# Thirty-two series of unused matmuls behind the last step: two row tiles with other column counts and places, then one row tile alone with other operands

## The chip, the core and the metric

The kernel runs on one core of one Trainium2 chip. A core has five engines with queues of their own: TensorE (PE in the profile; its weight loads stand apart as PEld), VectorE (DVE), ScalarE (ACT), GpSimd (POOL) and SyncE (SP, which here only issues DMAs). The metric is the device time of one execution in microseconds, the median of several runs. One run is also profiled, and all rows quoted below come from that one.

## The reference

The network has four residual layers on an image batch `x` of shape (4, 32, 32, 16). Three of them are alike: a group norm, then a layer in which every output pixel (i, j) has its own 3x3 convolution kernel.

```python
first   = einsum('ijyx,byxc->bijc', M, x)
shifted = conv(x, G[i, j], 3x3, 'SAME')            # for every one of 1024 pixels (i, j)
diff    = relu(x - shifted)
second  = einsum('ijyx,bijyxc->bijc', W, diff)
x       = x + first - second
```

With 1024 pixels, 16 output channels, four images and 1024 positions, `shifted` has 67 million elements for each of the three layers. That is where nearly all the time goes. The layer between the second and the third of them is a small interval-pooling network.

## The kernel before, in words

The batch is cut into two groups of two images, so there are six phases (three layers by two groups). A phase has eight chunks of 128 pixels, and a chunk has 32 steps, one for each of the 16 channels and two images. That makes 1536 steps. One step computes, for 128 pixels at once, the convolution at all 1024 positions of one image: a PSUM tile of 128 x 2 x 512 fp32, two banks, called `pc`.

The two halves of the tile (index `h`) belong to the left and right half of the image. Half `h` takes its operands from partitions 64h to 64h+63, so each matmul has 64 rows and 128 columns of weights, and the two halves work on two different row tiles of TensorE. The code issues them in turn, `h` = 0 and then `h` = 1, for each pair of operands (`products`, L629).

The operands are typed `float32r`, which the profile prints as f32. To come near fp32 precision, the inputs and weights are split into high and low parts, and seven products are accumulated in each step: two with `ib` and two with `ia` (`first_part`), then, after ScalarE has scaled the PSUM tile in place (L665), two with `iyz` and one with `im9` (`second_part`). The `ib` and `iyz` products have 512 columns, `ia` and `im9` 496 (the last or first image column is left out). After that, VectorE reads the PSUM tile, takes the minimum with zero, multiplies it by the pixel weights and sums it into an accumulator (L682). The first 16 steps (the units below `PLAIN`) take true fp32 operands `raw` in place of the split ones; such a product is two records in the profile.

The order is written out by hand (`manual_schedule`). The loop in `conv_layer` opens the first part of a step before the second part of the one before it, and lets background work in between (the preparation of weights in `prep_parts`, the group norm and gathers of the next phase in `behind`). PSUM tiles come in turn from four pairs of banks (`bank_pair`, tag `ps`, 4 buffers), so a new tile has to wait until the reader of the tile four allocations earlier is done. Weights of a unit of four channels lie in a tile `parts` of 2 x 3 x 4 x 128 columns; `ib[0]` holds 2048 columns of inputs of the first group.

At the end, the last `second_part` runs alone, VectorE adds the last accumulator to `X[1]` (L700), and SyncE sends the last slice of `X[1]` to the output (L904). Then all engines meet at a closing barrier.

## Time and profile before

| | us |
|---|---|
| median of 2 runs | 2481.81 (2479.29 and 2484.33) |
| time of the profiled execution | 2481.97 |
| its span, first to last instruction | 2480.3 |
| TensorE busy | 2458.5 (99%), 21906 matmuls |
| TensorE weight loads | 2074.2 (84%) |
| VectorE busy | 2086.0 (84%) |
| ScalarE busy | 1878.2 (76%) |
| GpSimd busy | 1579.3 (64%) |
| granted TensorE clock, mean | 1.000 |

Matmuls are pipelined: a record's duration covers its way through the array too, and it overlaps the next one's. How fast TensorE goes is therefore read from the distance between the starts of neighbouring matmuls and not from a matmul's duration. In the timeline view, neighbours of one kind are merged into one line (x4 is four matmuls, two on each row tile), and the first column is the start of the first of them.

### The profile page before, as it was taken

The page shows a single profiled execution, that of the slowest core. Times are in us where ns is not written, and L with a number is a line of the kernel's source. Part 1 is how long each engine was busy: PE and PEld are TensorE (multiplying, and loading weights), DVE is VectorE, ACT ScalarE, POOL GpSimd, SP SyncE. Part 2 cuts the span into 40 slices and gives each one's busy share as a digit, 9 for nine tenths or more (in the row PEclk, how much of TensorE's full clock was granted, in tenths as well). Part 3 has the DMA queues.
Part 4 walks back from the last instruction along what each step waited for, and adds up shares of the span by engine and source line. Part 5 has one row for each costly group of instructions (what it writes and reads, how often), then busy time and mean ns, then how long its engine had stood idle before and what let it go on. Part 6 is the DMA issues. An engine that isn't in the chain of part 4 may idle for free.

```text
span 2480.3 us, 58060 instructions
## 1 busy us (share of the span) xinstructions
PE 2458.5 (99%) x21906; PEld 2074.2 (84%) x21906; DVE 2086.0 (84%) x3617; ACT 1878.2 (76%) x2181; POOL 1579.3 (64%) x1750
## 2 busy tenths in 40 slices
PE   8999999999999999999999999999999999999999
PEld 4888888888888888888888989888989888888887
DVE  8888878888888888788898988899889888788887
ACT  3778767787777778677777777787777787677776
POOL 4766655667555667555567777586778676555552
PEclk9999999999999999999999999999999999999999
DMA  6556744465454457544454545574455477554442
GB/s 189 140 144 183 213 131 134 138 180 157 137 145 137 137 157 193 176 137 137 137 145 119 143 126 139 146 195 124 129 139 145 120 187 201 150 145 137 137 137 54
DMA packets 97673, 366.92 MB, mean 148 GB/s; under 512 B 26480, under 2 KB 31472, under 8 KB 97392
## 3 DMA queue, kind: packets, MB, share of 16 engines
q1 hardware_dynamic: 95696, 361.57, 52.9%
q8 instruction: 172, 2.82, 0.5%
q10 hardware_dynamic: 1568, 1.62, 0.3%
q14 instruction: 109, 0.89, 0.1%
q0 software_dynamic: 128, 0.02, 0.0%
HBM read 199.78 MB, written 1.02 MB: 81 GB/s over the span
## 4 chain that ended last, share of the span: by engine, by line
PE 94%; DVE 2%; DMA 2%; issue 1%; ACT 1%; POOL 0%; SPq 0%; ACTq 0%; DVEq 0%; POOLq 0%
PE pc L629 92%; DVE junk L682 1%; PE pf L427 1%; DMA parts<-parts 1%; ACT pc L665 0%; DMA raw<-in_xi 0%; DMA raw<-in_g 0%; DMA ia<-first 0%; PE ps_l L550 0%; DMA first<-in_g 0%; PE ps_r L563 0%; DVE tables L510 0%; DVE raw L848 0%; DVE upper_w L203 0%; SPq L302 0%
## 5 line engine op out<-in xcount | busy, mean ns | idle before, releaser
L682 DVE SCALAR_TENSOR_TENSOR junk<-pc,WT 128x1024 f32<-128x1024 f32 x1536 | 1880.0, 1224 | 363.6 <-PE pc L629 316.8
L665 ACT ACTIVATE pc<-pc 128x1024 f32<-128x1024 f32 x1520 | 1531.8, 1008 | 556.1 <-PE pc L629 531.6
L629 PE MATMUL pc<-ib,parts 64*128 64x512 f32 x6080 | 953.0, 387 | 4.7 <-DVE junk L682 2.9
L629 PE MATMUL pc<-iyz,parts 64*128 64x512 f32 x6080 | 950.3, 387 | 5.3 <-ACT pc L665 5.2
L629 PE MATMUL pc<-ia,parts 64*128 64x496 f32 x6080 | 928.5, 379 | 0.0
L629 PEld LDWEIGHTS pc<-ib,parts 64*128 64x128 f32 x6080 | 585.1, 184 | 109.3 <-DVE junk L682 8.5
L629 PEld LDWEIGHTS pc<-ia,parts 64*128 64x128 f32 x6080 | 587.6, 184 | 106.2
L629 PEld LDWEIGHTS pc<-iyz,parts 64*128 64x128 f32 x6080 | 586.2, 184 | 94.9 <-ACT pc L665 9.4
L629 PE MATMUL pc<-im,W 64*128 64x496 f32 x3072 | 606.4, 384 | 0.0
L237 POOL TENSOR_TENSOR parts<-raw,upper_w 128x512 fp32r<-128x512 f32 x190 | 249.0, 1311 | 496.3 <-DVE upper_w L203 447.3
L629 PEld LDWEIGHTS pc<-im,W 64*128 64x128 f32 x3072 | 297.8, 184 | 57.3 <-issue 3.6
L243 POOL CAST parts<-parts 32x512 fp32r<-32x512 f32 x380 | 231.2, 608 | 48.8 <-ACT parts L240 30.5
L238 POOL TENSOR_TENSOR W<-W,raw 128x512 fp32r<-128x512 f32 x190 | 246.9, 1300 | 7.8 <-ACT W L175 7.8
L241 POOL TENSOR_TENSOR parts<-parts 128x512 fp32r<-128x512 f32 x190 | 246.5, 1297 | 2.2 <-ACT parts L236 2.0
L245 POOL CAST parts<-upper_w 32x512 fp32r<-32x512 f32 x380 | 231.6, 609 | 22.8
L214 POOL TENSOR_TENSOR raw<-raw,ident 128x512 f32<-128x512 f32 x190 | 199.5, 1050 | 61.5 <-DMA raw<-in_g 36.6
L175 ACT ACTIVATE W<-raw,low_w 128x512 fp32r<-128x512 f32 x190 | 136.2, 717 | 9.2 <-DMA ia<-first 9.2
L682 DVE DVE_READ_ACCUMULATOR junk<-pc,WT 128x1 f32 x1536 | 127.8, 83 | 0.0
L236 ACT ACTIVATE parts<-upper_w 128x512 fp32r<-128x512 f32 x190 | 118.8, 625 | 4.8 <-DVE upper_w L203 4.7
L240 ACT CAST parts<-upper_w 128x512 fp32r<-128x512 f32 x190 | 116.6, 614 | 0.0
L697 POOL TENSOR_SCALAR acc<-acc 128x32 f32<-128x32 f32 x40 | 16.7, 417 | 136.5 <-DVE junk L682 134.6
L203 DVE TENSOR_SCALAR upper_w<-raw 128x512 int32<-128x512 int32 x190 | 85.2, 449 | 2.7 <-POOL raw L214 2.3
(139 smaller groups left out, 479.1 us busy)
## 6 DMA issues: line engine op xcount, KB each, us to landing
raw<-in_g SPq DMA_DIRECT2D x190, 768.0 KB, 7.1
parts<-parts SPq DMA_DIRECT2D x380, 384.0 KB, 5.0
WT<-in_w SPq DMA_DIRECT2D x48, 512.0 KB, 4.6
MT<-in_mt SPq DMA_DIRECT2D x24, 512.0 KB, 7.9
raw<-xs SPq DMA_DIRECT2D x120, 71.8 KB, 3.1
ib<-temp SPq DMA_DIRECT2D x40, 128.0 KB, 2.4
ia<-temp SPq DMA_DIRECT2D x80, 62.0 KB, 3.4
raw<-in_xi SPq DMA_DIRECT2D x3, 287.0 KB, 5.0
```

Source lines behind the costliest of these rows:

```text
L175: nc.scalar.activation(dst, src, AF.Copy, scale=mask[:, 1:2])
L214: eng.tensor_tensor(raws[u][:, s, at:to], raws[u][:, s, at:to], pick[s][:, f0 + at : f0 + to].unsqueeze(2).to_broadcast([P, to - at, P]), ...
L236: nc.scalar.activation(WD, high, AF.Copy, scale=-EPS)
L237: nc.gpsimd.tensor_tensor(WL, w8, high, ALU.subtract)
L238: nc.gpsimd.tensor_tensor(W9, W9.bitcast(F32), src[:, 2], ALU.add)
L240: nc.scalar.copy(WU, high)
L241: nc.gpsimd.tensor_tensor(WD, WD.bitcast(F32), WL.bitcast(F32), ALU.add)
L243: nc.gpsimd.tensor_copy(WU[hi], WL[lo].bitcast(F32))
L245: nc.gpsimd.tensor_copy(WL[lo], high[hi])
L629: nc.tensor.matmul(ps[:, h, at : at + n], lhsT=w[r], rhs=v[r] if n == NH else v[r][:, :n], start=first and k == 0, stop=k == len(pairs) - ...
L665: nc.scalar.activation(ps, ps, AF.Copy, scale=1.0 + EPS)
L682: nc.vector.scalar_tensor_tensor(junk, ps.rearrange("p h n -> p (h n)"), 0.0, chunks[n], op0=ALU.min, op1=ALU.mult, accum_out=accs[phase][ ...
```

## The change

After the output has been issued, 32 series of further matmuls are put into TensorE's queue. Each series takes a new PSUM tile and writes the same place of it 14 or 20 times (`start=True, stop=True`, so nothing accumulates). Nobody reads these tiles. The weights are slices of the last unit's `parts` tile, the moving operand is slices of `ib[0]`; both are left over from the kernel's own work.

- Twelve series (`aa` to `al`) of 20 pairs go to both row tiles in turn, as the kernel's own products do. They differ in the column count `n` (512, 480, 464, 448, 488, 504) and in which columns of `ib[0]` and `parts` the operands start.
- Twenty series (`ba` to `bt`) of 14 matmuls go to the first row tile alone. Among them are fewer weight columns (`m` of 64, 32, 96), weights whose access pattern repeats one column or half of them, moving operands whose pattern repeats 256, 64 or 16 columns or each column 16 times, the same operands each time, and column counts from 256 to 512.

In all that is 480 + 280 = 760 matmuls, each with its weight load. The rest of the program is left as it is, but for a list that keeps the last `parts` tile within reach.

```diff
+    all_parts = [None]
...
             parts = wpool.tile([P, 2, 3, FU, P], F32R, tag="parts", bufs=AHEAD + 1, name=f"parts_{u}")
             W9 = wpool.tile([P, FU, P], F32R, tag="W9", bufs=AHEAD + 1, name=f"W9_{u}")
+            all_parts[0] = parts
...
     second_part(*open_steps.pop(0))
     nc.sync.dma_start(out[1][:, NT - 1], X[1][:, NT - 1])
 
+    xf = ib[0].rearrange("p s b n -> p (s b n)")
+    wf = all_parts[0].rearrange("p a k f n -> p (a k f n)")
+
+    def more(name, n=NH, m=P, xs=(0, 512), ws=(0, 128), po=0, tiles=(0, 1), wc=None, xc=None, count=20):
+        ps = bank_pair(f"more_{name}_")
+        for k in range(count):
+            x0, w0 = xs[k % len(xs)], ws[k % len(ws)]
+            for h in tiles:
+                r = slice(64 * h, 64 * h + 64)
+                w, x = wf[r, w0 : w0 + m], xf[r, x0 : x0 + n]
+                if wc:
+                    w = bass.AP(w.tensor, w.offset, [list(w.ap[0])] + wc)
+                if xc:
+                    x = bass.AP(x.tensor, x.offset, [list(x.ap[0])] + xc)
+                nc.tensor.matmul(ps[:m, h, po : po + n], lhsT=w, rhs=x, start=True, stop=True)
+
+    one = dict(tiles=(0,), count=14)
+    more("aa")
+    more("ab", n=480)
+    more("ac", n=480, xs=(0,))
+    more("ad", n=480, xs=(0,), ws=(0,))
+    more("ae", n=480, xs=(0,), ws=(128,))
+    more("af", n=480, xs=(512,), ws=(0,))
+    more("ag", n=480, xs=(0, 256))
+    more("ah", n=480, xs=(0, 512, 1024, 1536), ws=(0, 256))
+    more("ai", n=464, xs=(0,), ws=(0,))
+    more("aj", n=448, xs=(0,), ws=(0,))
+    more("ak", n=488)
+    more("al", n=504)
+    more("ba", **one)
+    more("bb", m=64, **one)
+    more("bc", m=32, **one)
+    more("bd", m=96, **one)
+    more("be", wc=[[0, P]], **one)
+    more("bf", wc=[[64, 2], [1, 64]], **one)
+    more("bg", n=480, **one)
+    more("bh", n=464, **one)
+    more("bi", n=496, **one)
+    more("bj", n=448, **one)
+    more("bk", n=256, **one)
+    more("bl", n=384, **one)
+    more("bm", xc=[[0, 2], [1, 256]], **one)
+    more("bn", xc=[[0, 8], [1, 64]], **one)
+    more("bo", xc=[[0, 32], [1, 16]], **one)
+    more("bp", xc=[[1, 512 // 16], [0, 16]], **one)
+    more("bq", m=64, ws=(0, 64), **one)
+    more("br", xs=(0,), ws=(0,), **one)
+    more("bs", n=508, **one)
+    more("bt", n=498, **one)
```

## The prediction

> **What bounds the kernel now.** I read three views: the page for the bound, the timeline for the distance between matmuls, and the end of the timeline for what the added work can hide. On the page, the first line gives busy shares, the clock row gives the granted clock in 40 slices (9 is 90% or more), and the next line is the chain that ended last.

> ```profile
> PE 2458.5 (99%) x21906; PEld 2074.2 (84%) x21906; DVE 2086.0 (84%) x3617; ACT 1878.2 (76%) x2181; POOL 1579.3 (64%) x1750
> PEclk9999999999999999999999999999999999999999
> PE 94%; DVE 2%; DMA 2%; issue 1%; ACT 1%; POOL 0%; SPq 0%; ACTq 0%; DVEq 0%; POOLq 0%
> ```

> TensorE is the bound from end to end, at full clock. Work put behind its last matmul cannot hide behind another engine, except in the short tail. So the question is the price of one matmul of each kind. One steady step, TensorE alone, in the timeline (start, length, line, kind, count):

> ```profile
> 2471.39 0.38 PE L629 MATMUL pc<-im,W 64*128 64x496 f32 x2
> 2471.61 0.62 PE L629 MATMUL pc<-ib,parts 64*128 64x512 f32 x4
> 2472.06 0.60 PE L629 MATMUL pc<-ia,parts 64*128 64x496 f32 x4
> 2472.50 0.62 PE L629 MATMUL pc<-iyz,parts 64*128 64x512 f32 x4
> 2472.96 0.38 PE L629 MATMUL pc<-im,W 64*128 64x496 f32 x2
> ```

> The reader is to see starts: from 2471.39 to 2472.96, seven pairs pass in 1.57 us, four of 512 columns and three of 496. In the records' own start times (ns), a pair of 512 is followed after 226 or 227, a pair of 496 after 220 (1185 of 2050 `ia` to `ia` distances, the commonest value by far). The 16 columns between them cost 6.7 ns, so a column costs 1/2.4 ns, and each pair has 13.4 ns on top: 512/2.4 + 13.4 = 226.7, 496/2.4 + 13.4 = 220.1.

> This price belongs to **one tile**, not to the pair. In stretches where the two tiles run apart by 30 ns, the distances alternate 30 and 197 (512) or 30 and 190 (496): again 227 and 220 for each tile, whatever the other does.

> **The two-tile series.** Twelve series of 20 pairs. The column counts are 512 (`aa`), seven times 480 (`ab` to `ah`), 464, 448, 488 and 504, together 5776. So 20 x (5776/2.4 + 12 x 13.4) = 20 x (2406.7 + 160.8) = 51,350 ns: **51.3 us**. I cost other columns, shared columns and repeated weights at nothing, because `ia`, `ib`, `iyz` and `im` lie at different places and keep the same rule. A gain is bounded by the 13.4 ns (3.2 us in all); a loss has no row.

> **The one-tile series.** Twenty series of 14: twelve of 512 (6144), and 480, 464, 496, 448, 256, 384, 508 and 498 (3534), together 9678 columns. The trace before has one product on the first row tile alone, `ps_r` (L563), true fp32 in two passes:

> ```profile
> 1331.70 0.38 PE L629 MATMUL pc<-im,W 64*128 64x496 f32 x2
> 1331.70 0.40 PEld L563 LDWEIGHTS ps_r<-tables,r 64*128 64x128 f32 x2
> 1331.92 0.75 PE L563 MATMUL ps_r<-tables,r 64*128 64x352 f32 x2
> ...
> 1334.25 0.36 PE L563 MATMUL ps_r<-tables,r 64*128 64x231 f32 x1
> ...
> 1334.44 0.36 PE L563 MATMUL ps_r<-tables,r 64*128 64x231 f32 x1
> ```

> Its passes start 295 ns apart at 352 columns and 195 at 231, which is 1/1.2 ns a column plus 2 to 3. The fp32 products on both tiles (`raw`) start 430 apart at 512 columns: the same rate. So a tile alone is neither faster nor slower than one of two, in the one type where the trace shows both. The second weight load of `ps_r` starts 2 ns after the first pass and is covered by it.

> I therefore take the float32r rule for the lone tile as well: 14 x (9678/2.4 + 20 x 13.4) = 14 x (4032.5 + 268) = 60,210 ns: **60.2 us**. From below, the nearest rows bound the extra at 2.7 ns (`pf`, fp32, 256 columns: starts 216 apart against 213.3), which for all 520 slots (240 pairs, 280 singles) would take 5.6 us off. From above, two prices, both rivals below: the load in the open, and the fp32 column rate. I take 13.4, the row of the same type and shape.

> Smaller terms. A weight load that nothing covers moves the next matmul by 108 ns (at 2475.33 below: 335 instead of 227), so a load needs about 108; at 256 columns (`bk`) the slot is 120, and it still fits. Fewer weight columns (`bb`, `bc`, `bd`, `bq`) can only shorten the load; the change of tile width costs about 0.1 us where the trace has one (`im` to the 32-column `ps_l`, 317 instead of 220 ns), under 1 us for about seven. Repeating patterns (`be`, `bf`, `bm` to `bp`): the trace shows moving operands in runs of 16 (`raw`) at the common fp32 rate, but none that repeats. A form at half rate would cost 14 x 213 = 3 us, so 0 to 12 us if the four moving ones all did; I take 0, as short runs cost nothing.

> **Waits.** The four pairs of PSUM banks go round. The last four steps' readers end at about 2473.1, 2474.7, 2476.2 and 2477.6; the first four series begin at about 2476.1, 2480.7, 2485 and 2489, after each of them. From `ae` on, the previous writer of the buffer is TensorE itself, three series (10 us) back, and writing one place again is what every accumulating product does without a wait. Operands have long been there.

> **The end.** These are the last rows before:

> ```profile
> 2475.33 0.73 PE L629 MATMUL pc<-iyz,parts 64*128 64x512 f32 x4 [0.43 <-ACT pc L665]
> 2475.67 0.19 PEld L629 LDWEIGHTS pc<-im,W 64*128 64x128 f32 x2
> 2475.90 0.39 PE L629 MATMUL pc<-im,W 64*128 64x496 f32 x2
> 2476.15 0.08 DVE L682 DVE_READ_ACCUMULATOR junk<-pc,WT 128x1 f32 x1
> 2476.39 1.23 DVE L682 SCALAR_TENSOR_TENSOR junk<-pc,WT 128x1024 f32<-128x1024 f32 x1 [0.16 <-PE pc L629]
> 2477.54 0.08 DVE L682 DVE_READ_ACCUMULATOR junk<-pc,WT 128x1 f32 x1
> 2477.66 0.19 DVE L700 SCALAR_TENSOR_TENSOR X<-acc,X 128x32 f32<-128x32 f32 x1
> 2477.88 0.35 SPq L904 DMA_DIRECT2D out<-X  x1
> ```

> The output lands 1.4 us after its issue, at 2479.28, and the closing barrier takes the 1.0 us to 2480.3. The first added pair can start at 2475.90 + 0.22 = 2476.12. So VectorE's last reduction and the output (2476.12 to 2479.28, 3.2 us) lie beside added matmuls and drop from the path; if that cover were gone, they would cost those 3.2 us.

> **Sum.** 2476.12 + 51.35 + 60.21 = 2587.68; the last matmul's results come 0.2 us after its slot (length 0.39 in a slot of 0.22); plus 1.0 us of closing: span 2588.9. The profiled execution's time is 1.7 above its span (2481.97 against 2480.3), so **2590.5 us**, 108.5 above its own 2481.97, which is 0.16 above the median of the runs shown. The order of everything earlier is as before, so I take nothing from it.

> [...]

> **Rivals.**
> - *Lone loads in the open.* On two tiles, one tile's load could be covered by the other's stream, a cover that the lone tile lacks. Price: 280 x 108 = 30.2 us, so 2620.7. Against it: `ps_r`, and the tiles that run apart at an unchanged 227. For it: `ps_r` is the only lone row, with two passes of one product. Chance 0.07.
> - *A lone tile at half rate*, through the port that feeds it or a clock that drops when half of the array rests (the trace shows no long stretch of that kind). 14 x 9678/1.2 + 280 x 2.7 = 113.7 in place of 60.2: 2644. Chance 0.06.
> - *Some forms dearer, or waits between series*: four repeated forms at half rate 12 us, tile-width changes 1 us, so 2594 to 2606. Chance 0.13.
> - *Not slower: the unread matmuls are dropped* when the program is compiled, since no instruction reads a `more` tile. Then none of the 760 records appears, and the time is 2482. It decides at one point: whether an instruction without a reader is kept. In the trace nothing speaks for dropping, but it also has no unread tile. Chance 0.02.

> **Numbers.** The forecast, 2584 to 2594 by the bounds of the extra, has 0.70; the rest, 0.02, goes to cheaper ones. The range 2582 to 2606 takes in the forecast and the dearer forms (0.83), and leaves out open loads, half rate and dropping. A measurement of this kernel tells about 2% (50 us) from no change, so every case but dropping is slower: 0.98.

> **What would show it.** 760 more matmuls on TensorE's line of the page, about 111.6 us of new span after 2476. Right: 226.7 ns between `aa` pairs, 213.4 between the 480 ones, 227 between lone `ba` matmuls, and the output issued at 2477.9 as before. Wrong: lone matmuls about 335 apart (open loads) or 427 (half rate), a granted clock below 1 in the second half of the added stretch, or gaps at the starts of series.

## The result and the profile after

The changed kernel takes 2593.74 us, the median of 2 runs (2593.00 and 2594.49), against 2481.81 before: a ratio of 1.0448, with a 95% interval of 1.0430 to 1.0465. The forecast was 2590.5 us. The profiled execution takes 2593.0 us with a span of 2591.3.

From the page of the changed kernel, the rows that answer to those shown of before (busy shares, granted clock in 40 slices, the chain that ended last; the lines of the old code have moved down by one or two):

```profile
PE 2571.8 (99%) x22666; PEld 2166.7 (84%) x22666; DVE 2087.9 (81%) x3617; ACT 1878.4 (72%) x2181; POOL 1578.8 (61%) x1750
PEclk9999999999999999999999999999999999999999
PE 94%; DVE 2%; DMA 2%; issue 1%; ACT 1%; POOL 1%; SPq 0%; ACTq 0%; DVEq 0%; POOLq 0%
```

All 760 matmuls are there (21906 became 22666). The busy time of the other engines is unchanged within 2 us, and the clock is full in every slice.

The timeline of the changed kernel around the old end (start, length, engine, line, operation, count):

```profile
2476.79 0.39 PE L631 MATMUL pc<-im,W 64*128 64x496 f32 x2
2476.80 3.17 PEld L922 LDWEIGHTS more_aa__32783<-ib,parts 64*128 64x128 f32 x28
2477.02 3.36 PE L922 MATMUL more_aa__32783<-ib,parts 64*128 64x512 f32 x27
...
2478.55 0.19 DVE L702 SCALAR_TENSOR_TENSOR X<-acc,X 128x32 f32<-128x32 f32 x1
2478.77 0.35 SPq L906 DMA_DIRECT2D out<-X  x1
```

The first added matmul starts 0.23 us after the last `im` pair, where 0.22 lie between them in the steady steps. The last reduction and the output go on beside the added work. Two windows of the same trace, the twelve two-tile series and the twenty lone ones (length, then busy time and instruction count of each engine, granted clock, DMA share, GB/s; matmuls under way at a window's edge are counted too):

```profile
2477.02:2529.24 52.22, 52.22 (x482) 44.93 (x479) 1.53 (x5) 0.00 (x0) 0.00 (x0) 1.00 0.01 2
2529.24:2590.16 60.92, 60.92 (x282) 47.43 (x279) 0.00 (x0) 0.00 (x0) 0.00 (x0) 1.00 0.00 1
```

The forecast had 51.35 and 60.21. The lone series can be read one by one in TensorE's timeline; the distance from one line's start to the next, over 14, is the slot of one matmul:

```profile
2529.24 3.36 PE L922 MATMUL more_ba__33275<-ib,parts 64*128 64x512 f32 x14
2532.44 3.39 PE L922 MATMUL more_bb__33290<-ib,parts 64*64 64x512 f32 x14
...
2548.60 3.19 PE L922 MATMUL more_bg__33365<-ib,parts 64*128 64x480 f32 x14
2551.63 3.10 PE L922 MATMUL more_bh__33380<-ib,parts 64*128 64x464 f32 x14
...
2560.49 1.83 PE L922 MATMUL more_bk__33425<-ib,parts 64*128 64x256 f32 x14
2562.16 2.59 PE L922 MATMUL more_bl__33440<-ib,parts 64*128 64x384 f32 x14
...
2570.99 3.54 PE L922 MATMUL more_bo__33485<-ib,parts 64*128 64x512 f32 x14
2574.37 3.18 PE L922 MATMUL more_bp__33500<-ib,parts 64*128 64x512 f32 x14
2577.39 3.38 PE L922 MATMUL more_bq__33515<-ib,parts 64*64 64x512 f32 x14
```

From these, `ba` has 228 ns, `bg` 217, `bk` 120, and `bo` (runs of 16 that repeat) 242. `bp` (each column 16 times) has 216, less than any other of 512 columns. Two of the paired series, from the critical chain of the same trace (start, length, count):

```profile
2481.75 4.33 PE more_ab__32824 L922 x40
2512.08 4.20 PE more_ai__33111 L922 x40
```

Over their 20 pairs that is 216.7 ns at 480 columns and 210 at 464, the same as the lone `bg` and `bh`. Each series begins one slot after the last matmul of the one before (`bk` 203 ns after the last of `bj`, whose slot is 203; `bl` 120 after the last of `bk`), so the change of PSUM tile costs nothing here.

### The profile page after: what moved, and what is told of

It is laid out like the page before. It is cut to its first block, busy times and chain, and to the rows that moved or that the text cites. A ratio compares the mean times of both kernels' runs of the same rounds, so it can differ in the third digit from the quotient of the medians.

```text
span 2591.3 us, 59580 instructions
## 1 busy us (share of the span) xinstructions
PE 2571.8 (99%) x22666; PEld 2166.7 (84%) x22666; DVE 2087.9 (81%) x3617; ACT 1878.4 (72%) x2181; POOL 1578.8 (61%) x1750
## 4 chain that ended last, share of the span: by engine, by line
PE 94%; DVE 2%; DMA 2%; issue 1%; ACT 1%; POOL 1%; SPq 0%; ACTq 0%; DVEq 0%; POOLq 0%
PE pc L631 88%; DVE junk L684 1%; PE pf L429 1%; DMA raw<-in_g 1%; DMA parts<-parts 1%; DMA raw<-in_xi 0%; ACT pc L667 0%; PE more_aa__32783 L922 0%; PE more_al__33234 L922 0%; PE more_ak__33193 L922 0%; PE ps_l L552 0%; PE more_ah__33070 L922 0%; PE more_ae__32947 L922 0%; PE more_ag__33029 L922 0%; PE more_af__32988 L922 0%
```

## The experiments

In every kernel here the network itself is computed in full. Only the unused series change, or where they stand.

### Each half alone

```diff
     more("aa")
     ...
     more("al", n=504)
-    more("ba", **one)
-    ...
-    more("bt", n=498, **one)
```

> Only the twelve two-tile series are left (aa to al). My theory, a slot price for each matmul of a tile and a fixed cover of about 3 us by the tail: the series take the same 52.2 us as in the changed kernel (2477.02 to 2529.24), and the time is about 2481.8 + 52.2 - 3.0 = 2531 us. Rival (most of the added time comes from the lone series, the paired ones are partly free): under 2520 us.

> Only the twenty series on one row tile are left (ba to bt). My theory: the same 60.9 us as in the changed kernel, so about 2481.8 + 60.9 - 3.0 = 2540 us, lone 512-column matmuls 227 to 229 ns apart, granted clock 1.0. Rival (a tile alone is slower, or lowers the clock, once nothing on two tiles runs just ahead of it): 2560 us or more, and a clock below 1 in the stretch.

With the paired series alone the time is 2532.1 us (median of 4), 1.0193 of before (1.0178 to 1.0208); with the lone ones alone 2542.6, 1.0232 (1.0216 to 1.0248). The kernel before had a median of 2483.4 beside them. The series take 52.2 and 60.9 us in these traces too, and the plain lone 512-column matmuls (`ba`) are 226 to 236 ns apart, 229 in the mean, at full clock. Both halves cost what they cost in the changed kernel, and neither depends on the other.

### The series ahead of the last second part

```diff
+    ps = bank_pair("more_all_")
+    ... all 32 series, into this one tile ...
     second_part(*open_steps.pop(0))
     nc.sync.dma_start(out[1][:, NT - 1], X[1][:, NT - 1])
```

> All 32 series, but put ahead of the last step's second part, so that the last reduction and the output come after them; they share one PSUM tile. My theory (the tail is covered in the changed kernel and would be on the path here): from the start of the last but one step's im pair to the end of the span, 5.8 us before and 115.9 in the changed kernel, it is about 5.8 + 113.1 - 0.7 = 118.2 us, the 0.7 being the wait for ScalarE and the uncovered load that the series now hide. Rival (the tail hid nothing, the closing needs it anyway): 115.9 us or less.

The first two lines of this kernel's timeline below are the `im` pair of the last but one step and the first added pair, the others the end:

```profile
2474.12 0.38 PE L631 MATMUL pc<-im,W 64*128 64x496 f32 x2
2474.34 0.39 PE L920 MATMUL more_all__32773<-ib,parts 64*128 64x512 f32 x2
...
2588.41 1.23 DVE L684 SCALAR_TENSOR_TENSOR junk<-pc,WT 128x1024 f32<-128x1024 f32 x1 [112.57 <-PE pc L631]
2589.56 0.08 DVE L684 DVE_READ_ACCUMULATOR junk<-pc,WT 128x1 f32 x1
2589.68 0.19 DVE L702 SCALAR_TENSOR_TENSOR X<-acc,X 128x32 f32<-128x32 f32 x1
2589.89 0.35 SPq L957 DMA_DIRECT2D out<-X  x1
```

The span ends at 2592.3, so the distance is 118.2 us, against 115.9 in the changed kernel (2475.41 to 2591.3) and 5.8 before. The reduction and the output are on the path now, which makes the distance 2.3 us longer, although the last step's wait for ScalarE and its uncovered load are now hidden. In the kernel before, the `im` pair of the last but one step is this row:

```profile
2474.52 0.38 PE L629 MATMUL pc<-im,W 64*128 64x496 f32 x2
```

The next matmul starts at 2475.33, 0.59 us later than the usual 0.22, and the uncovered load takes another 0.11. With these 0.7 us, which were not measured apart, the cover is worth about 3.0 us, where the forecast had 3.2. In the time (1.0450 of before, 1.0433 to 1.0467) so small a term can't be seen.

### Loads, types and banks

```diff
+    one = dict(tiles=(0,), count=40)
+    more("ca", n=256, **one)
+    more("cb", n=192, **one)
+    more("cc", n=128, **one)
+    more("cd", n=128, m=32, **one)
+    more("ce", n=64, **one)
+    more("cf", n=64, m=32, **one)
+    more("cg", dt=F32, **one)
...
+    more("cl", banks=(0, 1), **one)
```

> Other series of 40 in place of the 32, to price loads and types. My theory (a lone tile's load of some 108 to 111 ns is covered by its own running matmul; 13.4 ns on top of N/2.4 for float32r): lone 256 columns 120 ns, 192 columns 111, 128 columns 111 with 128 weight columns and 67 with 32, 64 columns 111 and 40; pairs of 256 and 128 columns like the lone ones; true fp32 of 512 columns 430 for each of the two passes, alone and in pairs; two banks in turn 227. Rival (loads in the open): lone 256 columns 228, 192 columns 201, 128 columns 175. Rival (a tile alone streams at half rate): lone fp32 over 800. Rival (the 13.4 ns comes from writing one PSUM bank again): two banks in turn 216.

Windows of this trace for lone 256, the first part of 192, then 128, 128 with 32 weight columns, 64, 64 with 32, true fp32 alone (80 passes), pairs of 128, and two banks in turn:

```profile
2479.99:2484.78 4.79, 4.79 (x43) 4.79 (x40) 1.53 (x5) 0.00 (x0) 0.00 (x0) 1.00 0.02 3
2484.78:2488.33 3.55, 3.55 (x34) 3.55 (x33) 0.00 (x0) 0.00 (x0) 0.00 (x0) 1.00 0.00 0
2490.02:2498.50 8.48, 8.48 (x41) 8.48 (x41) 0.00 (x0) 0.00 (x0) 0.00 (x0) 0.50 0.00 0
2498.50:2502.77 4.27, 4.27 (x41) 4.27 (x42) 0.00 (x0) 0.00 (x0) 0.00 (x0) 0.50 0.00 0
2502.77:2511.26 8.49, 8.49 (x42) 8.49 (x41) 0.00 (x0) 0.00 (x0) 0.00 (x0) 0.50 0.01 2
2511.26:2513.40 2.14, 2.14 (x42) 2.14 (x42) 0.00 (x0) 0.00 (x0) 0.00 (x0) 0.50 0.00 0
2513.40:2580.10 66.70, 66.70 (x83) 26.11 (x80) 0.00 (x0) 0.00 (x0) 0.00 (x0) 0.50 0.00 0
2637.00:2641.60 4.60, 4.60 (x86) 4.60 (x83) 0.00 (x0) 0.00 (x0) 0.00 (x0) 1.00 0.00 0
2641.65:2650.80 9.15, 9.15 (x42) 7.23 (x41) 0.00 (x0) 0.00 (x0) 0.00 (x0) 1.00 0.01 2
```

Distances in the text are between starts of neighbours. Where pairs follow a lone series, their first matmuls on the idle second tile start beside the last lone ones, so a window that is cut there is a little short (66.70 us for 80 passes of 853 ns).

At full clock, lone 256 takes 120 ns and lone 192 takes 111: the load is covered. Below some 230 columns it is the bound (an estimate: there N/2.4 + 13.4 falls to the 108 to 111 ns of a load). Loads in the open (228 and 201) are refuted.

Then something came that my theory did not have: 3.5 us into the 192-column series the clock halves, and no lone series brings it back (0.50 in every window from 2490.02 to 2580.10). At half clock, 128 and 64 columns take the same 213 ns with 128 weight columns, about twice the 108 to 111 of a load at full clock, and 107 and 53 with 32, which is N/1.2: there the load is covered as well. The 853 ns of lone fp32 look like the rival's half rate, but they belong to the clock: at full clock a later run has 429. Pairs of 128 columns take 111 ns at full clock, like a lone load, and the two passes of fp32 on both tiles 429 each. Two banks in turn take 227 in most places and 229 in the mean, so the extra is not from writing one bank again.

### What the extra 13.4 ns are

```diff
+    more("da", **one)
+    more("db", xc=[[1, 256], [0, 2]], **one)
...
+    more("df", xc=[[0, 512]], **one)
+    more("dg", xc=[[2, 512]], xs=(0, 512), **one)
...
+    more("dm", xc=[[1, 128], [0, 4]], **both)
```

> Series of 40 lone 512-column matmuls with other patterns of the moving operand (and three on both tiles), to see what the 13.4 ns are that my forecast added to N/2.4. Theory now, after the changed kernel's bp (each column 16 times, 215.6 ns): they belong to the fetch of the moving operand, so a pattern that fetches fewer different columns loses them: each column 2, 4, 8, 16 or 512 times goes from 228 down to 216, alone and on both tiles, with plain or repeated weights; runs that repeat (32 columns) or leave gaps (16 of 18) do not gain: 227 or more, 8-column runs 240 or more. Rival (they belong to the change of weights): 227 in all but repeated weights.

Windows for the plain series, each column twice, one column 512 times, every second column, repeated runs of 32, and each column four times on both tiles:

```profile
2474.83:2483.93 9.10, 9.10 (x42) 7.36 (x40) 1.51 (x5) 0.00 (x0) 0.00 (x0) 1.00 0.01 2
2483.93:2492.56 8.63, 8.63 (x41) 7.44 (x40) 0.00 (x0) 0.00 (x0) 0.00 (x0) 1.00 0.01 2
2518.46:2527.10 8.64, 8.64 (x42) 7.44 (x40) 0.00 (x0) 0.00 (x0) 0.00 (x0) 1.00 0.00 0
2527.10:2545.21 18.11, 18.11 (x42) 11.54 (x40) 0.00 (x0) 0.00 (x0) 0.00 (x0) 0.58 0.00 0
2545.21:2562.25 17.04, 17.04 (x41) 13.02 (x40) 0.00 (x0) 0.00 (x0) 0.00 (x0) 0.50 0.00 0
2622.54:2631.17 8.63, 8.63 (x83) 7.44 (x82) 0.00 (x0) 0.00 (x0) 0.00 (x0) 1.00 0.01 2
```

Over 40 matmuls, the plain series takes 227.5 ns each and every one at full clock that uses each column several times in a row 215.8, which is 512/2.4 + 2.5, alone and on both tiles. Repeated weights do not help (`be` in the changed kernel, 232). So most of the 13.4 ns is there where every column is a new one and gone where a column is used again at once, and it does not go with the weights. Every second column costs 451 ns from the start, still at full clock, and 453 to 454 after the clock has halved, so this distance does not follow the clock. It is about twice the plain 227.5; why, no run shows.

That series also halved the clock after 3 us, and the ones behind it (repeated runs of 32, runs of 16 with gaps, runs of 8, and repeated columns with repeated weights) went at 427 ns = 512/1.2, whatever their pattern. What these patterns cost at full clock was therefore not measured here; the changed kernel has 227 for repeated runs of 64 columns (`bn`) and 242 for runs of 16 (`bo`). At half clock the extra is gone too.

### When the clock drops

```diff
+    more("ea", n=256, count=120, **one)
+    more("eb", **both)
+    more("ec", n=224, count=120, **one)
...
+    more("ee", count=60, **one)
...
+    more("eg", dt=F32, count=12, **one)
...
+    more("ei", n=96, tiles=(0, 1), count=120)
...
+    more("em", n=192, m=32, count=120, **one)
```

> Longer series between stretches on both tiles, to see how near the forecast was to its rival of a halved clock, which a run with lone 192-column matmuls has shown. Theory: the clock follows the share of the array that streams (columns streamed per slot, times half for a lone tile), and drops somewhere between the 36% of lone 192 columns and the 44% of lone 256: lone 256 (120 in a row) stays at 1.0, lone 512 (60 in a row) stays at 1.0 at 47%; lone 224 at 40% is open; true fp32 alone (25%) drops to 0.5 and shows 853 ns a pass; pairs of 96 columns in load-bound slots of 111 ns (36%) drop as well; lone 192 with 32 weight columns in slots of 93 ns (43%) stays. Rival (a lone tile drops the clock by itself, whatever it streams, if it goes on long enough): lone 512 and lone 256 drop, pairs of 96 stay.

Windows for lone 256, lone 224, lone 512, lone fp32, pairs of 96, and lone 192 with 32 weight columns:

```profile
2474.26:2488.29 14.03, 14.03 (x120) 14.03 (x118) 1.53 (x5) 0.00 (x0) 0.00 (x0) 1.00 0.01 2
2495.47:2508.54 13.07, 13.07 (x120) 13.06 (x119) 0.00 (x0) 0.00 (x0) 0.00 (x0) 1.00 0.00 1
2515.70:2528.63 12.93, 12.93 (x60) 10.49 (x59) 0.00 (x0) 0.00 (x0) 0.00 (x0) 1.00 0.00 0
2536.10:2545.12 9.02, 9.02 (x24) 3.93 (x23) 0.00 (x0) 0.00 (x0) 0.00 (x0) 1.00 0.00 0
2552.78:2574.76 21.98, 21.98 (x242) 21.91 (x240) 0.00 (x0) 0.00 (x0) 0.00 (x0) 0.60 0.01 1
2607.19:2617.70 10.51, 10.51 (x120) 10.51 (x119) 0.00 (x0) 0.00 (x0) 0.00 (x0) 1.00 0.01 2
```

The clock falls for pairs of 96 columns, on both tiles, and stays for every lone series here (distances between starts: 227 ns for lone 512, 429 for a pass of lone fp32; the windows are short for the reason given above). "A tile alone drops the clock" is refuted. What falls together is the share of the array that streams, worked out from these distances: 36% for lone 192 columns in 111 ns (192/2.4/111, times half) and for pairs of 96 (96/2.4/111), against 42% (lone 224 in 112 ns), 44% (lone 256), 45% (lone 192 in 88 ns) and 47% (lone 512), which stay.

A rival would sort all these series in the same way: the share of time in which anything streams, whatever the rows (72% for lone 192, 36% for pairs of 96, against 83% and more). Two rows speak against it. In the loads run (row 2637.00), both tiles start their 128 columns within 5 ns of each other from the fourth pair on, every 111 ns, so something streams for 48% of the time, and the clock stays at 1.00 over all of the 4.6 us. In that trace the clock changed at 2488.33, 2583.91, 2621.45 and 2635.11: 28, 11 and 4 times 3.41 us lie between them, and these pairs fill 3.1 of the 3.4 us before 2641.94, where the next such moment would lie (an estimate from those four). And at a halved clock a lone tile that streams without a break (427 ns = 512/1.2) does not bring it back, where pairs do (113 us and 5.2 us in the last two runs below). So rows count as well as time in these runs. That rests on one stretch of 4.6 us, and the limit is known only as lying between 36% and 42%.

One point was wrong. I had true fp32 alone at 25% and falling; it stays at 1.0 for 9 us, with passes 429 ns apart, as on two tiles. If a pass that takes 1/1.2 ns a column is counted as streaming all that time, the share is 50%. By the same count lone fp32 of 96 columns in the loads run has 36% (80 ns in 112), and there the clock fell after 4.3 us. The half-rate rival is refuted with it: lone fp32 costs 429 at full clock.

### Counts and places

```diff
+    one = dict(tiles=(0,), count=30, xs=(0,), ws=(0,))
+    more("ga", n=320, **one)
...
+    more("gi", n=480, **one)
+    more("gj", n=488, **one)
+    more("gk", n=496, **one)
...
+    one["xs"] = (4,)
+    more("ha", **one)
```

> Series of 30 lone matmuls with the column count alone changed (320 to 512), then 512 columns with other starts of the moving operand and of the weights. My forecast: N/2.4 + 13.4 for each. After the changed kernel, where 480 columns took 216.7 and 488 took 225.5: theory that the extra depends on the column count alone, 13 at 496 and 512, 17 at 464 and 480, 22 at 488, and not on the places. Rival (the places make it: operands that change from one matmul to the next): 488 with one place falls to 217, and 512 with changing places rises to 228.

Windows for 320, 480, 488, 496 and 512 columns from column 0, and 512 columns from column 4, each 30 matmuls:

```profile
2480.95:2485.34 4.39, 4.39 (x32) 4.39 (x30) 1.53 (x5) 0.00 (x0) 0.00 (x0) 1.00 0.02 4
2524.75:2531.26 6.51, 6.51 (x31) 5.51 (x30) 0.00 (x0) 0.00 (x0) 0.00 (x0) 1.00 0.00 0
2531.26:2538.02 6.76, 6.76 (x32) 5.57 (x30) 0.00 (x0) 0.00 (x0) 0.00 (x0) 1.00 0.00 0
2538.02:2544.72 6.70, 6.70 (x32) 5.54 (x30) 0.00 (x0) 0.00 (x0) 0.00 (x0) 1.00 0.01 2
2558.22:2565.04 6.82, 6.82 (x31) 5.52 (x30) 0.00 (x0) 0.00 (x0) 0.00 (x0) 1.00 0.00 0
2565.04:2571.99 6.95, 6.95 (x31) 5.53 (x30) 0.00 (x0) 0.00 (x0) 0.00 (x0) 1.00 0.00 0
```

Above N/2.4 the mean distances between starts leave 13 to 14 ns at 320 to 400 columns, 15 to 17 from 416 to 480, 22 at 488, 17 at 496, and 14 at 512. The 488 columns keep their 225 ns with one place, so the count makes most of it. Places matter too, by a few ns: 496 from one place takes 223 where alternating places took 220 in the changed kernel, and 512 starting at column 4 takes 232; but 512 with changing places (0 and 512) stays at 227.5, as from one place. Neither theory holds alone, and what sets the pattern stays open. At stake are 3 to 9 ns of 220.

### The lone series at a halved clock

```diff
+    more("zz", xc=[[2, 512]], tiles=(0,), count=24)
+    more("zy", count=30)     # the second kernel only
     more("ba", **one)
     ...
```

> The twenty lone series, unchanged, but behind 24 lone matmuls that read every second column, which in an earlier run went with a halved clock that no lone stream behind it raised again. Theory (a lone tile keeps a full clock that it finds, but cannot raise a halved one): the twenty series run at a granted clock of 0.5 and take N/1.2 each, 14 x 9678/1.2 = 112.9 us in place of 60.9, which is the rival of my forecast at its price. Rival (the clock comes back within some microseconds of steady lone matmuls): 65 us or less.

> The same, with 30 pairs of 512 columns on both tiles between the every-second-column matmuls and the twenty lone series. Theory: the pairs bring the clock back within some 5 us, and the lone series take 60.9 us at 1.0 again. Rival (something else than the clock was halved): still over 100 us.

Both kernels leave out the twelve paired series. The twenty unchanged lone series, behind the every-second-column matmuls:

```profile
2492.70:2605.60 112.90, 112.90 (x281) 83.35 (x279) 0.00 (x0) 0.00 (x0) 0.00 (x0) 0.50 0.00 0
```

The same with 30 pairs between them (the pairs first, then the series):

```profile
2490.72:2500.67 9.95, 9.95 (x64) 7.77 (x63) 0.00 (x0) 0.00 (x0) 0.00 (x0) 0.74 0.01 2
2500.67:2561.57 60.90, 60.90 (x281) 47.42 (x279) 0.00 (x0) 0.00 (x0) 0.00 (x0) 1.00 0.00 1
```

The same 280 matmuls take 112.9 us where they find a halved clock, and 60.9 where pairs have raised it first. In 113 us of unbroken lone matmuls the clock does not come back; on both tiles it does 5.2 us into the 30 pairs.

## Why the prediction was right

**The price of a slot on one tile** was the step that carried the forecast, and it held: 227 to 228 ns for lone 512 columns, 220 for 496, 120 for 256. That the price belongs to a tile and not to the pair is borne out by equal counts: 216.7 ns at 480 columns and 210 at 464, in pairs and alone. The places that the seven paired series of 480 change cost nothing, as forecast: all take 216.7.

**Covered loads** held: 120 ns for lone 256 columns and 111 for 192, where loads in the open would have made 228 and 201. By what means a load goes on beside a matmul of its own tile, no run here shows.

**The extra** was a little small. It is the term of the sum that was mis-sized: 13.4 ns came from 496 and 512 columns, and the series have 12.9 to 22 with other counts, 28.5 for `bo` and 2.3 for `bp`. Over all series this makes 113.14 us in place of 111.56. These 1.6 us, and 0.9 us by which the earlier stretch ended later in this execution, are the whole difference of 2.5 us between 2590.5 and the profiled 2593.0. At full clock the float32r rows come down to some 2.5 ns over N/2.4 only where a column repeats (215.8 ns for 512); the fp32 rows have it without that (429 ns a lone pass of 512 columns, 512/1.2 + 2.3; in the kernel before, the passes of `ps_r` at 231 columns lie 197 to 198 ns apart, not the 195 of the forecast, so 5 over).

**Forms dearer** was a rival priced at up to 12 us. Of the repeating patterns only `bo` cost more to speak of (0.2 us over 14 matmuls), and `bp` was the cheapest of all. The change of tile width cost nothing that shows: the first 64-column matmul of `bb` starts 226 ns after the last of `ba`. Fewer weight columns, which I held could only shorten the load, made the slot of 512 columns 1 to 4 ns longer (229.8 ns with 96, 230.5 with 64 and 232.3 with 32, against 228.5 with 128), although the load itself did get shorter (its records last 158, 131 and 104 ns, against 184).

**The waits, the tail and the closing** held: no gap between series, the output issued beside the added work, 1.4 us from the last matmul's start to the end of the span. The cover was shown by taking it away, at about 3.0 us for the 3.2 of the forecast.

**Dropping** the unread matmuls did not happen; all 760 records are in the trace.

## What to carry to other kernels

Price a matmul by the distance between starts of neighbours of its own type and shape on the same tile, at the same clock; where two tiles run apart by some ns, their distances show whether the price belongs to a tile or to a pair. Before costing a stretch that uses half of the array, work out which share of it streams (here 36% halved the clock and 42% did not) and which clock the stretch finds. A lone tile held a full clock for 60.9 us but did not raise a halved one in 113 us, so thin work goes behind dense work, or has some dense work put ahead of it.

## What the runs showed that I had not expected

- The clock halved within 3 to 5 us (3.0 to 4.8) while TensorE had matmuls without a pause: at 36% of the array streaming (lone 192 columns, pairs of 96) and at 24% (every second column), not at 42% and above.
- The extra of a float32r matmul above N/2.4 falls from 13 to 2.5 ns when each column is used at least twice in a row, and is gone at half clock (427 ns = 512/1.2).
- Reading every second column takes 451 ns for 512 columns at full clock, twice the plain 227, and 453 at half clock.
- Slots that the load of 128 weight columns bounds grew with the clock: 213 ns at half clock (128 and 64 columns), 111 at full clock (lone 192, pairs of 128).
- Fewer weight columns made a lone slot of 512 columns longer, not shorter: 231 ns with 64 and 232 with 32, against 228 with 128. Why was not tried.
